# A decoder layer's state-space scan: input products one unit further ahead, units in another order

## The chip, the core and the metric

The kernel runs on one core of a Trainium2 chip. The core has a matrix engine (PE, TensorE), three elementwise engines (DVE or VectorE, ACT or ScalarE, POOL or GpSimd), and SP (SyncE), which here only issues transfers. Each engine works through its own instructions in order, and semaphores make one wait for another. SBUF and PSUM are the on-chip memories of 128 partitions[...]. The metric is the device time of one execution in microseconds. The kernel before took 1646.77 us, the median of 3 runs (1646.59 to 1649.17).

## The reference

One decoder layer on 4 sequences ("batches") of 512 positions and 512 features, in float32. It has three residual parts: a Mamba block, an int8-like quantized expert ("xattn") per sequence, and a mixture of 16 experts with a shared one. The change touches the Mamba block, whose core is a recurrence over time for 1024 channels with 16 states each:

```python
delta = softplus(einsum('dr,blr->bld', dt_proj_weight, dt) + dt_proj_bias)
A = -exp(A_log)
def step(h, inputs):
    d_t, B_t, C_t, u_t = inputs
    dA = exp(d_t[..., None] * A)
    h = h * dA + (d_t * u_t)[..., None] * B_t[:, None, :]
    y = einsum('bdn,bn->bd', h, C_t)
    return (h, y)
...
y = ys + u * D
y = y * silu(z)
return einsum('md,bld->blm', out_proj_weight, y)
```

Here u is a short convolution and silu of the first half of an input projection, z its second half, and dt, B and C are projections of u.

## The kernel before

**Units.** The 1024 channels of a batch go in NC = 8 chunks of 128 (`c`). In a chunk a *unit* `(g, p)` is the work on one of NG = 4 groups of states (4 states each) and on one half `p` of the chunk, that is two quarters of 32 channels. 32 channels by 4 states fill the 128 partitions; the two quarters lie beside each other, so that a unit is 128 partitions by 2 x 512 positions. A chunk has NU = 8 units, a batch 64, the kernel 256. `UNITS` (line 39) is their order: before, the pair of groups 0 and 1 on half 0, then both on half 1, then groups 2 and 3 likewise.

**What a unit does.** `spread` (690) copies delta and delta*u of a half from the tile `dd` to a tile `rep`, 32 rows to 128, by two transfers of 512 KB on SP; there are three rep buffers. `unit_inputs` (701) makes, on ACT, the decays `da` (two exponentials into PSUM, two buffers) and, on POOL, the product `bu` of B and delta*u (two buffers). `unit_scan` (714) is the recurrence itself, one scan on DVE over `da` and `bu`. `unit_out` (720) multiplies by C on DVE into a tile `h` (five buffers). `state_sums` (727) sums the 4 states of each channel by small matmuls with a 0/1 matrix `sel` into the PSUM tile `py`, which a matmul with the `skip` matrix (u*D) opens. `gated` (756) multiplies py by the gate `gzl` of the chunk, which `gate` (750) has loaded.

**Order of the work.** `scan_batch` (1653) writes the instructions slot by slot, a slot for each unit n. At its start it writes the inputs of unit n+1; at n = 4 the skip matmul and the sums of groups 0 and 1, at n = 0 those of groups 2 and 3 of the chunk before, whose `gated` follows at n = 1. Then come the scan, the output and, in three places (`more`, before the scan, before the output, and at the end of the slot), steps of the work beside.

**The work beside.** It is written as generators whose steps say what they wait for: `delta` (650, softplus for the chunk after next; four POOL operations of 128x512), `front` (475, layer norm, input projection, convolution and gates of the next batch; on POOL three additions a chunk at 502), the gates of batch 0 (`first_gates`, 613), the `back` of the batch before (763: output projection, quantized expert, shared expert and routing), and in the last batch the experts. The class `Pace` (133) keeps a clock for each engine while the instructions are being written. `clear` (222) lets a step be written only if its engine's clock is at most `BEHIND` past DVE's, and its inputs are ready at most `SLACK` past it; the calls before the scan and before the output add 3500 and 1200 ns for engines other than DVE. For POOL, SLACK is -300 and BEHIND 500 ns.

**Deadlines.** The list `copies` holds the rep halves to come: half 1 of the next chunk from n = 5, half 0 of the chunk after it from n = 7. A half is spread once its delta is over, and at n = 6 (half 0) and n = 7 (half 1) a delta that is not over is forced: `end` (1637) writes its steps until it is. The skip matrix of the chunk after next is loaded at n = 5. In the last chunk of a batch the tiles `bc` (B and C of a group, one buffer each) are loaded for the next batch, groups 0 and 1 at n = 4 and groups 2 and 3 at n = 7. Transfers on SP are issued in the order written, and one that must wait for its buffer holds those behind it.

Of the kernel before, what the change touches and what calls it, by code (L numbers as in the profile page):

```python
# [8 lines left out]
F32 = mybir.dt.float32  # L9
# [10 lines left out]
P = 128  # L20
B = 4
L = 512
# [4 lines left out]
NC = DI // P  # L27
# [3 lines left out]
CH = 32  # L31
# [4 lines left out]
NP = 2  # L36
NU = NG * NQC // NP

UNITS = [(g + i, p) for g in range(0, NG, 2) for p in range(NQC // NP) for i in range(2)]

GROUPS = [(0, 2), (2, 2)]

# [90 lines left out]
class Pace:  # L133
# [6 lines left out]
    TABLES = {"Exp": 0, "Tanh": 0, "Silu": 1, "Ln": 2}  # L140


    SLACK = {"DVE": 200, "Activation": 700, "Pool": -300, "PE": 3500, "SP": 500}
    BEHIND = {"DVE": 0, "Activation": 1500, "Pool": 500, "PE": 5000, "SP": 4000}

    def __init__(self, nc):
        self.nc, self.seen, self.table, self.queue = nc, 0, None, 0
# [95 lines left out]
def following(b, c, n):  # L243

    return (b, c + n) if c + n < NC else (b + 1, c + n - NC)
# [24 lines left out]
class Kernel:  # L270
# [271 lines left out]
    def first_front(self, sb, bank):  # L542

        nc, st = self.nc, self.state[0]
        xnT = self.xnT0
        for j in range(4):
            self.load_win(0, sb, j)
        for _ in self.layernormed(0, sb, bank, xnT):
            pass
        nc.sync.dma_start(self.wx_sb, self.wx)  # L550
        nc.sync.dma_start(self.wdt_sb, self.wdt)
        pj = {}
        pdt = bank.take([P, L])
        pbc = bank.take([P, L])


        pairs = [(b, self.fsideT[b], 0, k) for b in range(B) for k in (0, 2)]
        pairs += [(b, self.ctxwT[b], NK, 0) for b in range(B)]
        each = -(-len(pairs) // NC)
        held = {}  # L560

        def columns(c):
            for i in range(c * each, min((c + 1) * each, len(pairs))):
                b, w, _, k = pairs[i]
                held[i] = self.sb.tile([P, NP, L], F32, name="h", bufs=5)
                nc.sync.dma_start(held[i], w[k * P : (k + 2) * P, :].rearrange("(k p) n -> p k n", k=2))

        def largest(c):
            for i in range(c * each, min((c + 1) * each, len(pairs))):
                b, _, first, k = pairs[i]  # L570
                out = self.amw[:, b, first + k : first + k + 2]
                nc.vector.tensor_reduce(out, held.pop(i), AX.X, ALU.max, apply_absolute_value=True)

        def product(c):
            pj[c] = self.in_proj(0, bank, xnT, c)
            self.load_win(0, sb, c + 4)
            columns(c)

        def conv(c):
            cw = self.convw_sb  # L580
            u = self.u_tile(0, c)
            nc.scalar.activation(u, pj[c], AF.Copy, scale=cw[:, c, DC - 1 : DC])
            for j in range(1, DC):
                nc.vector.scalar_tensor_tensor(
                    u[:, j:], pj[c][:, : L - j], cw[:, c, DC - 1 - j : DC - j], u[:, j:], ALU.mult, ALU.add
                )
            bank.done(pj[c])

        def silu(c):
            nc.scalar.activation(st["u"][c], st["u"][c], AF.Silu, scale=2.0)  # L590
            largest(c)

        def sums(c):
            self.x_proj_of(st, pdt, 0, c)
            self.x_proj_of(st, pbc[: 2 * DS], 1, c)

        for _ in staged(range(NC), product, conv, silu, nothing, sums):
            pass
        flat = self.amw.rearrange("p b k -> p (b k)")
        nc.vector.reciprocal(flat, flat)  # L600
        nc.gpsimd.tensor_scalar_min(flat, flat, 1.0 / EPS_Q)
        st["dt"] = self.sb.tile([P, L], F32, name="dt", bufs=1)
        nc.scalar.copy(st["dt"], pdt)
        bank.done(pdt)
        rows = sb.tile([2 * DS, L], F32, name="rows", bufs=1)
        nc.scalar.copy(rows, pbc[: 2 * DS])
        bank.done(pbc)
        nc.sync.dma_start(self.rows_d[0], rows)
        self.done.add(("rows", 0))
        for g in range(NG):  # L610
            self.scan_bc(0, g)
# [86 lines left out]
            )  # L698
        st["rep"][c, p] = rep

    def unit_inputs(self, b, c, n):

        nc, st = self.nc, self.state[b]
        g, p = UNITS[n]
        rep = st["rep"][c, p]
        da = self.pscan.tile([P, NP, L], F32, name="da", bufs=2)
        for i in range(NP):
            q = c * NQC + p * NP + i
            nc.scalar.activation(da[:, i, :], rep[:, i, 0, :], AF.Exp, scale=self.a_sb[:, q, g : g + 1])  # L709
        bu = self.sb.tile([P, NP, L], F32, name="bu", bufs=2)  # L710
        nc.gpsimd.tensor_mul(bu, st["bc"][0, g].unsqueeze(1).to_broadcast([P, NP, L]), rep[:, :, 1, :])  # L711
        st["da"][c, n], st["bu"][c, n] = da, bu

    def unit_scan(self, b, c, n):
        st = self.state[b]
# [4 lines left out]
    def unit_out(self, b, c, n):  # L720
        st = self.state[b]
        g, p = UNITS[n]
        h = self.sb.tile([P, NP, L], F32, name="h", bufs=5)
        self.nc.vector.tensor_mul(h, st["da"].pop((c, n)), st["bc"][1, g].unsqueeze(1).to_broadcast([P, NP, L]))  # L724
        st["h"][c, g, p] = h

    def state_sums(self, b, c, g0):

        nc, st = self.nc, self.state[b]
        if g0 == 0:  # L730
            st["py"] = self.pscan.tile([P, L], F32, name="py", bufs=1)
            nc.tensor.matmul(st["py"], self.skips.pop((b, c)), st["u"][c], start=True, stop=False)
        py = st["py"]
        for g in range(g0, g0 + 2):
            for q in range(NQC):
                nc.tensor.matmul(  # L736
                    py[q * CH : (q + 1) * CH, :],
                    self.sel,
                    st["h"][c, g, q // NP][:, q % NP, :],
                    start=False,  # L740
                    stop=(g == NG - 1),
                )

    def skip(self, b, c):

# [799 lines left out]
    def run(self, ctx):  # L1545
# [21 lines left out]
        with tc.tile_pool(name="front", bufs=2) as fsb:  # L1567
            self.fsb = fsb
            self.first = ExitStack()
            sb = self.first.enter_context(tc.tile_pool(name="first", bufs=1))  # L1570
            self.xnT0 = sb.tile([P, NK, L], F32, name="xnT0", bufs=1)
            self.bank.add(self.pscan, "py")
            self.first_front(sb, self.bank)
            self.bank.names.remove((self.pscan, "py"))
            self.deltas, self.copies = {}, []
            for c in range(2):
                self.steps_of(0, c)
                self.skip(0, c)
            self.end(self.deltas[0, 0])
            for p in range(NQC // NP):  # L1580
                self.spread(0, 0, p)
            self.copies.append((0, 1, 0))
            self.fronts = Steps(self.pace, (w for b in range(1, B) for w in self.front(b)))
            self.unit_inputs(0, 0, 0)
            pool = ctx.enter_context(ExitStack())
            routed = Steps(self.pace, self.first_experts())
            backs = Steps(self.pace, self.backs(pool))
            backs.due = lambda slot: BACK_STEPS * (slot - NC * NU) / DUE
            self.fronts.due = lambda slot: FRONT_STEPS * slot / DUE
            self.scan_batch(0, [Steps(self.pace, self.first_gates(sb))])  # L1590
            for b in range(1, B - 1):
                self.scan_batch(b, [backs])
            assert self.fronts.over
# [52 lines left out]
    def finish(self, b, n):  # L1646

        if n == 0:
            self.state_sums(b, NC - 1, NG // 2)
        elif n == 1:  # L1650
            self.gated(b, NC - 1)

    def scan_batch(self, b, beside):

        self.started.add(b)
        for i in range(NC * NU):
# [3 lines left out]

            nb, nc = following(b, c, (n + 1) // NU)
            if nb < B:
                self.unit_inputs(nb, nc, (n + 1) % NU)

            if n == 4:
                self.state_sums(b, c, 0)
            if n == 0 and c:
                self.state_sums(b, c - 1, NG // 2)
            if b and not c:
                self.finish(b - 1, n)  # L1670
            self.more(beside, 3500)
# [3 lines left out]
            self.more(beside, 1200)  # L1675
            self.unit_out(b, c, n)
            if n == 2:
                self.gate(b, c)
                self.steps_of(*following(b, c, 2))

            if n == 5:
                self.skip(*following(b, c, 2))
                self.copies.append((*following(b, c, 1), 1))
            if n == 7:
                self.copies.append((*following(b, c, 2), 0))
            while self.copies:
                db, dc, p = self.copies[0]
                if db < B:
                    late = (db, dc) == following(b, c, 1) and n == NU - 2 + p or (db, dc) == (b, c)
                    if late:  # L1690
                        self.end(self.deltas[db, dc], [*self.deltas.values(), self.fronts, *beside])
                    elif not self.deltas[db, dc].over or self.pace.ready(self.state[db]["dd", dc]) > self.pace.engine["DVE"]:
                        break
                    self.spread(db, dc, p)
                self.copies.pop(0)
            if b + 1 < B and c == NC - 1 and n in (4, 7):
                for g in range(2):
                    self.scan_bc(b + 1, g + (n == 7) * 2)
            self.more(beside, 0)
# [67 lines left out]
```

## Time and profile before

All times are microseconds.

| what | value |
|---|---|
| median of 3 runs | 1646.77 |
| the profiled execution's own time | 1661.86 |
| its span, first to last instruction | 1659.9 |
| mean granted TensorE clock (share of full speed) | 0.844 |
| first scan starts, last scan starts | 90.7, 1335.0 |
| scans begin in batch 0, 1, 2, 3 | 90.7, 353.6, 671.9, 998.6 |
| DVE busy, 88 to 345 (257 long) | 231.3 |
| POOL busy, 88 to 345 | 228.8 |
| DVE busy, 345 to 680, 680 to 1010, 1010 to 1340 | 271.2, 275.3, 271.5 |
| POOL busy, the same stretches | 264.3, 248.2, 235.3 |
| DVE and POOL busy, 1340 to 1660 | 108.2, 143.3 |

The profile is of one execution, so sums are made against its own span. Its groups of instructions are given by line, engine and tile, as out<-in; "idle before" is the time that the engine stood idle just before such an instruction, with what ended the wait. Idle time of an engine that doesn't set the end costs nothing. In the rows of slices the span is cut in 40 equal parts, and a digit is the busy share in tenths. The page's chain of waits covers only the last 38 us, after which it finds no earlier link; it says nothing of the scan stage.

### The profile page before, as it was taken

To read this page: it belongs to the slowest core of one execution; us is meant where nothing else is said; L and a number is where in the kernel's file an instruction comes from. 1 tells how busy PE (TensorE), PEld (TensorE's weight loads), DVE (VectorE), ACT (ScalarE), POOL (GpSimd) and SP (SyncE) were. 2 spreads that over 40 slices of the span, in tenths; PEclk is the share of its full clock that TensorE was granted. 3 is DMA by queue.
4 is the path that set the end of the run, shared out by engine and by line. 5 is a ranking of instruction groups with operands and counts; after the bars stand their busy time and mean duration, and the time that the engine had idled before them with its cause. 6 is when DMAs were issued, how large, how long until landed. Compare 5 with 4: busy or idle time off the path is not lost. (4 is left out here: it accounts for less than half of the span.)

```text
span 1659.9 us, 15722 instructions
## 1 busy us (share of the span) xinstructions
PE 1207.7 (73%) x4552; PEld 584.8 (35%) x4552; DVE 1193.2 (72%) x1250; ACT 941.3 (57%) x1592; POOL 1130.7 (68%) x940
## 2 busy tenths in 40 slices
PE   6848777557866767898867885866667899668980
PEld 2213222112332323333423432343424347434760
DVE  4369999898867888778878898877778934352312
ACT  3376786755757778555787762567575414520330
POOL 1178999886767988676787874777788644126464
PEclk9978888768877887899978897987777999868995
DMA  5575655675233556665335658555567464168956
GB/s 192 154 162 126 141 110 111 130 189 110 74 90 78 135 120 163 161 203 143 78 84 127 172 137 293 138 158 133 130 184 204 120 260 146 65 230 292 342 213 216
DMA packets 109658, 262.22 MB, mean 158 GB/s; under 512 B 16192, under 2 KB 20416, under 8 KB 109504
## 3 DMA queue, kind: packets, MB, share of 16 engines
q1 hardware_dynamic: 93120, 204.50, 47.4%
q0 software_dynamic: 16448, 56.65, 9.8%
q8 instruction: 40, 0.66, 0.2%
q14 instruction: 50, 0.41, 0.1%
HBM read 168.55 MB, written 45.88 MB: 129 GB/s over the span
## 5 line engine op out<-in xcount | busy, mean ns | idle before, releaser
L711 POOL TENSOR_TENSOR bu<-bc,rep 128x1024 f32<-128x1024 f32 x256 | 602.2, 2358 | 169.8 <-DVE da L718 140.2
L718 DVE TENSOR_TENSOR_SCAN da<-da,bu 128x1024 f32<-128x1024 f32 x256 | 586.2, 2290 | 105.2 <-POOL bu L711 74.4
L709 ACT ACTIVATE da<-rep,a_sb 128x512 f32<-128x512 f32 x512 | 352.7, 690 | 261.2 <-DVE h L724 229.4
L724 DVE TENSOR_TENSOR h<-da,bc 128x1024 f32<-128x1024 f32 x256 | 312.3, 1220 | 19.6 <-PE py L736 9.2
L736 PE MATMUL py<-h,sel 128*32 128x512 f32 x1024 | 166.1, 687 | 50.2 <-DVE h L724 50.1
L1223 POOL DMA_INDIRECT wx<-in_wexp,wrow x62 | 63.0, 1016 | 79.9 <-PE bank L1513 22.9
L446 PE MATMUL bank_g<-xnT,win 128*128 128x512 f32 x192 | 100.2, 670 | 8.6 <-ACT tap L498 6.0
L502 POOL TENSOR_TENSOR u<-u,tap 128x511 f32<-128x511 f32 (+2 forms) x72 | 91.3, 1268 | 18.1 <-ACT tap L498 15.9
L446 PE MATMUL bank_b<-xnT,win 128*128 128x512 f32 x160 | 82.1, 661 | 24.6 <-ACT sp_r L669 15.2
L736 PEld LDWEIGHTS py<-h,sel 128*32 128x32 f32 x1024 | 31.1, 119 | 164.4 <-issue 83.3
L1467 POOL DMA_INDIRECT xs<-xn_d,tok x62 | 64.3, 1038 | 20.9 <-issue 19.2
L446 PE MATMUL bank_a<-xnT,win 128*128 128x512 f32 x128 | 63.2, 640 | 3.0 <-DVE gz L411 2.4
L446 PEld LDWEIGHTS bank_g<-xnT,win 128*128 128x128 f32 x192 | 40.5, 219 | 63.0 <-issue 51.2
L446 PEld LDWEIGHTS bank_b<-xnT,win 128*128 128x128 f32 x160 | 32.9, 213 | 72.9 <-issue 38.5
L680 POOL TENSOR_TENSOR sp_e<-sp_e,dd 128x512 f32<-128x512 f32 x32 | 40.7, 1272 | 26.2 <-ACT dd L675 26.1
L1261 POOL DMA_INDIRECT yg<-y_d,pos x32 | 33.3, 1041 | 23.9 <-DMA y_d<-ys 9.5
L1504 ACT ACTIVATE hs<-bank 128x128 f32<-128x128 f32 x24 | 6.6, 276 | 67.5 <-PE bank L1498 36.5
L1271 DVE SCALAR_TENSOR_TENSOR xr<-yg,topw,xr 128x512 f32<-128x512 f32 x32 | 23.7, 750 | 28.8 <-DMA yg<-y_d,pos 28.5
L791 PE MATMUL bank_b<-wout,u 128*128 128x512 f32 x64 | 36.1, 724 | 10.7 <-ACT tap L498 6.2
L1498 PE MATMUL bank<-xT,wx 128*128 128x128 f32 x352 | 43.1, 276 | 0.6 <-issue 0.6
L1498 PEld LDWEIGHTS bank<-xT,wx 128*128 128x128 f32 x352 | 41.3, 192 | 4.3 <-issue 3.5
L411 DVE SCALAR_TENSOR_TENSOR hs<-hs,bank 128x128 f32<-128x128 f32 x24 | 6.8, 284 | 50.1 <-ACT hs L1504 35.7
(422 smaller groups left out, 2439.4 us busy)
## 6 DMA issues: line engine op xcount, KB each, us to landing
rep<-dd SPq DMA_DIRECT2D x128, 512.0 KB
win<-in_win SPq DMA_DIRECT2D x64, 256.0 KB
x<-xr SPq DMA_DIRECT2D x48, 256.0 KB
xr<-x SPq DMA_DIRECT2D x48, 256.0 KB
y_d<-ys SPq DMA_DIRECT2D x48, 256.0 KB
bc<-rows_d SPq DMA_DIRECT2D x32, 256.0 KB
gz_d<-gz SPq DMA_DIRECT2D x32, 256.0 KB
gzl<-gz_d SPq DMA_DIRECT2D x32, 256.0 KB
```

The lines of the kernel that those rows point to most:

```text
L446: nc.tensor.matmul(pj, win[:, k, :], xnT[:, k, :], start=(k == 0), stop=(k == NK - 1))
L502: nc.gpsimd.tensor_add(u[:, j:], u[:, j:], v[j][:, j:])
L680: nc.gpsimd.tensor_sub(e, e, du)
L709: nc.scalar.activation(da[:, i, :], rep[:, i, 0, :], AF.Exp, scale=self.a_sb[:, q, g : g + 1])
L711: nc.gpsimd.tensor_mul(bu, st["bc"][0, g].unsqueeze(1).to_broadcast([P, NP, L]), rep[:, :, 1, :])
L718: self.nc.vector.tensor_tensor_scan(daf, daf, buf, 0.0, ALU.mult, ALU.add)
L724: self.nc.vector.tensor_mul(h, st["da"].pop((c, n)), st["bc"][1, g].unsqueeze(1).to_broadcast([P, NP, L]))
L736: nc.tensor.matmul(py[q * CH : (q + 1) * CH, :], self.sel, st["h"][c, g, q // NP][:, q % NP, :], start=False, stop=(g == NG - 1),)
L791: nc.tensor.matmul(po[t], st["u"][c][:, t * P : (t + 1) * P], wout[c], start=(c == part[0]), stop=(c == part[-1]),)
L1223: nc.gpsimd.indirect_dma_start(out=ws[s], out_offset=None, in_=self.wexp, in_offset=bass.IndirectOffsetOnAxis(ap=wrow[:, s : s + 1], axis= ...
L1467: nc.gpsimd.indirect_dma_start(out=xs[s], out_offset=None, in_=xn_d, in_offset=bass.IndirectOffsetOnAxis(ap=tok[:, s : s + 1], axis=0), bo ...
L1498: nc.tensor.matmul(ph[:, i, :], w[:, o : o + P], xT[:, k, :], start=(k == 0), stop=(k == NK - 1))
```

## The change

The order of units becomes group by group, each on both halves. `unit_inputs` is split: `unit_decays` (ACT) still runs one unit ahead; `unit_products` (POOL) runs two ahead, in three bu buffers. h has four buffers instead of five, each tile of the same 4 KB a partition. The sums of a group are written at the second slot after its first unit (n = 2, 4, 6, and n = 0 of the next chunk). The planner's two numbers for POOL are raised. Deadlines move: late deltas are forced at n = 5 and 6, half 0 of the chunk after next is listed from n = 6, and half 1 at n = 5 as before; the bc tiles of groups 0 and 1 are loaded at n = 3. Two loops write the steps on which a load depends until they are done: gates of batch 0, and `rows` of the next batch.

```diff
-UNITS = [(g + i, p) for g in range(0, NG, 2) for p in range(NQC // NP) for i in range(2)]
+UNITS = [(g, p) for g in range(NG) for p in range(NQC // NP)]
...
-    SLACK = {"DVE": 200, "Activation": 700, "Pool": -300, "PE": 3500, "SP": 500}
-    BEHIND = {"DVE": 0, "Activation": 1500, "Pool": 500, "PE": 5000, "SP": 4000}
+    SLACK = {"DVE": 200, "Activation": 700, "Pool": 2500, "PE": 3500, "SP": 500}
+    BEHIND = {"DVE": 0, "Activation": 1500, "Pool": 3500, "PE": 5000, "SP": 4000}
...
-                held[i] = self.sb.tile([P, NP, L], F32, name="h", bufs=5)
+                held[i] = self.sb.tile([P, NP, L], F32, name="h", bufs=4)
...
-    def unit_inputs(self, b, c, n):
+    def unit_decays(self, b, c, n):
...
-        bu = self.sb.tile([P, NP, L], F32, name="bu", bufs=2)
-        nc.gpsimd.tensor_mul(bu, st["bc"][0, g].unsqueeze(1).to_broadcast([P, NP, L]), rep[:, :, 1, :])
-        st["da"][c, n], st["bu"][c, n] = da, bu
+        st["da"][c, n] = da
+
+    def unit_products(self, b, c, n):
+        nc, st = self.nc, self.state[b]
+        g, p = UNITS[n]
+        bu = self.sb.tile([P, NP, L], F32, name="bu", bufs=3)
+        nc.gpsimd.tensor_mul(
+            bu, st["bc"][0, g].unsqueeze(1).to_broadcast([P, NP, L]), st["rep"][c, p][:, :, 1, :]
+        )
+        st["bu"][c, n] = bu
...
-        h = self.sb.tile([P, NP, L], F32, name="h", bufs=5)
+        h = self.sb.tile([P, NP, L], F32, name="h", bufs=4)
...
-    def state_sums(self, b, c, g0):
+    def state_sums(self, b, c, i):
...
-        for g in range(g0, g0 + 2):
-            for q in range(NQC):
...
+        for q in range(NQC):
+            h = st["h"][c, i, q // NP][:, q % NP, :]
+            nc.tensor.matmul(py[q * CH : (q + 1) * CH, :], self.sel, h, start=False, stop=(i == NG - 1))
...
-            self.unit_inputs(0, 0, 0)
+            self.unit_decays(0, 0, 0)
+            for n in range(2):
+                self.unit_products(0, 0, n)
...
-                self.unit_inputs(nb, nc, (n + 1) % NU)
-
-            if n == 4:
-                self.state_sums(b, c, 0)
+                self.unit_decays(nb, nc, (n + 1) % NU)
+            nb, nc = following(b, c, (n + 2) // NU)
+            if nb < B:
+                self.unit_products(nb, nc, (n + 2) % NU)
+
+            if n and n % 2 == 0:
+                self.state_sums(b, c, n // 2 - 1)
             if n == 0 and c:
-                self.state_sums(b, c - 1, NG // 2)
+                self.state_sums(b, c - 1, NG - 1)
...
             if n == 2:
+                while b == 0 and ("gate", b, c) not in self.done:
+                    beside[0].go()
...
             if n == 5:
+                self.copies.append((*following(b, c, 1), 1))
                 self.skip(*following(b, c, 2))
-                self.copies.append((*following(b, c, 1), 1))
-            if n == 7:
+            if n == 6:
                 self.copies.append((*following(b, c, 2), 0))
...
-                    late = (db, dc) == following(b, c, 1) and n == NU - 2 + p or (db, dc) == (b, c)
+                    late = (db, dc) == following(b, c, 1) and n == NU - 3 + p or (db, dc) == (b, c)
...
-            if b + 1 < B and c == NC - 1 and n in (4, 7):
+            if b + 1 < B and c == NC - 1 and n in (3, 7):
+                while ("rows", b + 1) not in self.done:
+                    self.fronts.go()
```

More of the change, by code (lines that the diff above doesn't have):

```diff
@@ L722, in unit_out @@
         g, p = UNITS[n]
-        h = self.sb.tile([P, NP, L], F32, name="h", bufs=5)
+        h = self.sb.tile([P, NP, L], F32, name="h", bufs=4)
         self.nc.vector.tensor_mul(h, st["da"].pop((c, n)), st["bc"][1, g].unsqueeze(1).to_broadcast([P, NP, L]))
         st["h"][c, g, p] = h
-    def state_sums(self, b, c, g0):
+    def state_sums(self, b, c, i):
         nc, st = self.nc, self.state[b]
-        if g0 == 0:
+        if i == 0:
             st["py"] = self.pscan.tile([P, L], F32, name="py", bufs=1)
@@ L733, in state_sums @@
         py = st["py"]
-        for g in range(g0, g0 + 2):
-            for q in range(NQC):
[L736 to L742, printed above, removed]
+        for q in range(NQC):
+            h = st["h"][c, i, q // NP][:, q % NP, :]
+            nc.tensor.matmul(py[q * CH : (q + 1) * CH, :], self.sel, h, start=False, stop=(i == NG - 1))
     def skip(self, b, c):
@@ L1648, in finish @@
         if n == 0:
-            self.state_sums(b, NC - 1, NG // 2)
+            self.state_sums(b, NC - 1, NG - 1)
         elif n == 1:
```

## The prediction

> **What bounds the kernel now.** I read the busy shares first, then the slices, then the groups with their idle time, then the table of who waited for whom, and last the timeline around single waits.
>
> ```profile
> PE 1207.7 (73%) x4552; PEld 584.8 (35%) x4552; DVE 1193.2 (72%) x1250; ACT 941.3 (57%) x1592; POOL 1130.7 (68%) x940
> ...
> DVE  4369999898867888778878898877778934352312
> ...
> POOL 1178999886767988676787874777788644126464
> ...
> L711 POOL TENSOR_TENSOR bu<-bc,rep 128x1024 f32<-128x1024 f32 x256 | 602.2, 2358 | 169.8 <-DVE da L718 140.2
> L718 DVE TENSOR_TENSOR_SCAN da<-da,bu 128x1024 f32<-128x1024 f32 x256 | 586.2, 2290 | 105.2 <-POOL bu L711 74.4
> ...
> L724 DVE TENSOR_TENSOR h<-da,bc 128x1024 f32<-128x1024 f32 x256 | 312.3, 1220 | 19.6 <-PE py L736 9.2
> ```
>
> The scan stage runs from the first scan at 90.7 us to the last at 1335.0 us, three quarters of the span. A unit costs DVE 2.29 + 1.22 = 3.51 us, 256 of them 898.6 us. Summed over 88 to 1340 us, 1252 us long, DVE is busy 1049.2, POOL 976.5, PE 913.9, ACT 824.9. So DVE sets the stage, and what can be won is in its 203 us of idle time. From the starts of the scans the four batches take 263, 318, 327 and 340 us: 4.1 us a unit in batch 0, 5.0 to 5.3 after.
>
> ```profile
> ACT da L709 <- DVE h L724: 229.4, 109, 11.7
> POOL bu L711 <- DVE da L718: 140.2, 78, 10.3
> ...
> DVE da L718 <- POOL bu L711: 74.4, 29, 27.4
> ...
> DVE da L718 <- ACT da L709: 29.4, 17, 4.4
> ...
> POOL bu L711 <- DMA rep<-dd: 25.2, 6, 9.2
> ```
>
> These rows are total, number, longest. POOL waits 78 times for a free bu buffer, and all the same DVE waits 29 times for bu: POOL is early on the average and late at times, which is what a deeper buffer is for. But the 74.4 us are not all to be had. I took each of these scans from the timelines and asked when the decays of the same unit were ready. Where bu came last DVE lost 69.4 us; decays alone would have kept 39.7 of them, 25.6 at the very first scan (the wait of 27.4, for the first rep) and 9.9 at 472.40 us. The other cases leave **26 us: 9 in batch 0, in bits of 0.3 to 1.7, and 17 after it**, of which 5.3 are at 1146.77 and 0.9 at 1244.45.
>
> **The change part by part.**
>
> *Products two ahead.* The 256 products stay, at 2.36 us; each is issued a slot earlier, past the POOL side work of that slot. The bound is 0 to −26 us. The planner's own allowance tells how much of the small waits goes. Before, ahead of a scan it lets POOL stand 3.5 + 0.5 us past DVE and then writes one more addition (1.27) and the product (2.36): 7.6 us, against two units of 3.51, so 0.6 us late. That is what the trace has in batch 0 (waits of 0.50, 0.53, 0.55, 0.60, 0.62, 0.69). After: 3.5 + 3.5 + 1.27 + 2.36 = 10.6 against 10.5, 0.1 late. I take 7 of batch 0's 9, and half of the later 17, whose causes are stalls in POOL's own queue, which the wider SLACK (2.5 us for an input not yet ready, where it was −0.3) also makes likelier. **−15.5 us.**
>
> Here a rule of the Trainium skill speaks against the change. "Perfetto Trace Analysis", section "Identifying the Most-Contended Engine", has the engine of the highest occupancy worked on first. That is PE or DVE here, and the change takes no instruction from either: by the rule the sum is 0. By the waits, DVE's gaps are ended by an engine with 68% occupancy, and −15.5 stands. I go by the rows, since occupancy doesn't tell which engine is late.
>
> *Four buffers for h, sums every two units.* DVE's waits for h on the sums are 9.2 us in three places (0.72, 3.11, 5.35), all at unit 5 of a chunk, one slot after the eight sums were written. Now a reused h has its sums two slots back; a slot more is 3.5 us at least, and 8.8 at the longest. All three go: **−9** (bound 0 to −9.2). PE pays: 64 more groups, each with a bubble (0.76 us in the timeline ahead of the first sum), 49 us, beside 338 us of PE idle in the stage. PE is near full (56.6 of 60 us) only from 720 to 780: 49 × 60/1252 = **+2.4**. And PE, which runs in order, sits at the sums until DVE's h is done: 50.1 us of matmul idle now, at 64 places, then at 128. Behind it stand the in_proj and back products, and DVE waits for such products (all but py) for 48 us in the stage. Bounds 0 and +48; most of this work is written only when it is due, so near the low end: **+5**. In the startup two h tiles a step are loaded; with four buffers each load would find its buffer already read (the loads at 31.03 reuse what was reduced by 30.6): 0, since the margin is 0.4 us at its least; if it fails, a win load behind them on SP waits about a microsecond.
>
> *Units by state group.* Both halves of rep are now in use to the end of a chunk. Half 1 of the next chunk takes the buffer of half 0, whose last reader was unit 5 and is now unit 6; and it is first read by unit 1, whose product is written in slot 7, where it was unit 2, in slot 1 of the next chunk. So its transfer starts a slot later and is wanted two slots sooner. I call T5 the start of scan 5. Unit 6's two decays (1.42 us) run after h of unit 4, so the buffer is free at T5 + 1.5.
>
> ```profile
> 460.93 7.81 SPq L696 DMA_DIRECT2D rep<-dd  x4
> ...
> 468.11 0.69 ACT L709 ACTIVATE da<-rep,a_sb 128x512 f32<-128x512 f32 x1 [9.59 <-DMA rep<-dd]
> 469.94 2.02 ACT L709 ACTIVATE da<-rep,a_sb 128x512 f32<-128x512 f32 x3 [1.14 <-DMA rep<-dd]
> ...
> 472.40 2.30 DVE L718 TENSOR_TENSOR_SCAN da<-da,bu 128x1024 f32<-128x1024 f32 x1 [11.64 <-POOL bu L711]
> ```
>
> In this timeline (start, duration, operation, idle before it and what ended it) a half is whole 9.0 us after its issue; two more cases that POOL waited for give 9.4 and 10.4 (issues 1250.5 and 625.3, products 1259.88 and 635.71). Then the product: ready at T5 + 1.5 + 9.0..10.4 + 2.4 = T5 + 12.9 to 14.3. Scan 1 of the next chunk is at T5 + 4 slots: 16.4 us in batch 0, over 20 later. The room is **2.1 to 3.5 us in batch 0 and 6 to 8 us after**. "DMA: Bandwidth & Descriptors", section "Specifications", gives 435 GB/s as the ceiling into SBUF: an estimate from it for the 1.05 MB is 2.4 us, and some 8 us of room even in batch 0. The rows say four times that, and decide: the half comes just in time. Old issues of half 1 lie in slots 4 and 5 but for four later ones out of 32; each of those I charge a microsecond: **+4**, bounds 0 and +22 (below).
>
> SP is also rid of a wait: the skip load ahead of half 1 waited for the chunk's skip matmul, now two slots sooner.
>
> ```profile
> SPq L748 <- PE py L732: 67.8, 15, 14.4
> ```
>
> *Deadlines.* A late delta is forced at the end of slot 5 for half 0, was 6. The stall at 472.40 came of it: transfer in slot 7. One slot sooner takes 4 to 5 us off: **−5** (0 to −11). At startup unit 1 needs half 1, there at 93.81, plus its product 2.36: 96.2 instead of 95.38, **+0.8**. The bc loads a slot sooner wait on SP for h of unit 3 up to a slot, three times in all, with two slots of room for the reader: 0, up to +5 if SP's queue behind them holds a rep. The two new loops (gate in batch 0, rows) do nothing where the step is done: rows left at slots 50, 56 and 49 of their batches, wanted at 59: 0 (but see rival B). Decays stay one ahead, so DVE's 29.4 us on ACT stay.
>
> *Sum*: −15.5 − 9 + 2.4 + 5 + 4 − 5 + 0.8 = **−17.3 us** on the profiled execution, 1661.9 us with 2 us around its span, which is 0.9% above the runs' median. Scaled: 1646.8 − 17.1 = **1630 us**. The tail after 1340 us waits for the last batch in any case, so the gain passes through to it.
>
> **The rivals.**
>
> A, *rep half 1 becomes the wait* (slower). Place: SP's queue ahead of that transfer in slots 5 and 6, where the win loads stand. SP's waits for PE's in_proj before a win load are 40 with a total of 239 us, 6.0 each. If one of these stands ahead of half 1 at each chunk end, batch 0 loses 7 × (6.0 − 2.8) = 22 us, the others nothing: −15 + 22 gives about 1655 us. Nothing is left of the gain from 5 us of delay on; beyond 7 us the 24 later chunks pay too. For it: the room worked out above. Against it: in batch 0 half 1 left SP at 212.4, 245.7 and 279.0, just as its buffer came free, with SP waiting for nothing else.
>
> B, *forced side work*: with PE held at the sums, the front or the gates of batch 0 come late, and the loops write steps that are not ready, on which the in-order engines sit. For it: such loops cost only where a schedule misses its deadlines, and rows of batch 2 had three slots to spare. Some 10 us at each of three batch ends, less half the gain: 1662 us.
>
> C, *the lead is spent*: the planner fills it with POOL work that waits for its inputs, and ACT's decays, one ahead, end the waits that bu ended. 0 of the 15.5, the rest as above: −2, 1645 us.
>
> **Numbers.** A measurement here tells some 0.2% (3.3 us) from no change. Forecast 0.48, A 0.22, B 0.17, C 0.13 (0.09 within 0.2%, 0.04 slower by unlisted costs). Faster 0.48, same 0.09, slower 0.43. The forecast's own range is 1612 (all 26 and the 11) to 1643 (POOL a quarter, PE +20). With A to C: 1610 to 1668; that leaves out a strong A with over 8 us of delay and B at its worst.
>
> **What would show it.** POOL's bu row: idle before it on DVE's scan falls from 140, DVE's wait for bu falls from 74 to under 50, its wait for h on py to about 0. PE's wait at the sums grows past 50. POOL's wait for rep rises from 25; if it passes 60 with DVE's scans at unit 1 of a chunk behind it, A holds. DVE's wait on ACT's decays over 40 would be C. Batch 0 should take about 256 us instead of 263. It is wrong if batch 0 gets longer, or if the scan stage shortens and the tail after the last scan grows by as much.

## The result, and the profile after

The changed kernel took 1696.3 us (median of 4, 1691.7 to 1703.9), the kernel before 1646.8: a ratio of **1.030, interval 1.027 to 1.033**. Forecast was 1630, range 1610 to 1668. It is slower by 49.5 us. The profiled execution's span is 1689.6 us.

The page of the changed kernel: slices of DVE, then the groups that answer to those shown of before.

```profile
DVE  4379898989798788879567785987787853344412
...
L717 POOL TENSOR_TENSOR bu<-bc,rep 128x1024 f32<-128x1024 f32 x256 | 600.0, 2356 | 207.6 <-DMA rep<-dd 115.3
L726 DVE TENSOR_TENSOR_SCAN da<-da,bu 128x1024 f32<-128x1024 f32 x256 | 586.2, 2290 | 103.9 <-ACT da L709 55.0
...
L732 DVE TENSOR_TENSOR h<-da,bc 128x1024 f32<-128x1024 f32 x256 | 312.5, 1221 | 14.3 <-PE py L744 2.1
L744 PE MATMUL py<-h,sel 128*32 128x512 f32 x1024 | 211.2, 733 | 96.2 <-DVE h L732 96.0
```

And the row of the sums in the kernel before:

```profile
L736 PE MATMUL py<-h,sel 128*32 128x512 f32 x1024 | 166.1, 687 | 50.2 <-DVE h L724 50.1
```

On DVE and POOL the same work takes the same busy time, while PE's sums, now in twice as many groups, are busy 45 us longer. What has changed most is who ends the waits. POOL used to wait for scans (140.2 us), which is being early; now it waits most for the copied halves `rep`. The scans used to wait most for bu and now do for the decays. The table of waits (total, times, longest) of the same kernel:

```profile
POOL bu L717 <- DMA rep<-dd: 115.3, 27, 13.4
POOL bu L717 <- DVE da L726: 77.2, 29, 10.1
...
DVE da L726 <- ACT da L709: 55.0, 35, 4.7
DVE da L726 <- POOL bu L717: 46.4, 12, 27.3
...
ACT da L709 <- DMA rep<-dd: 36.3, 16, 9.4
```

From the first scan to the last output the stage went from 1249.0 to 1296.5 us; DVE's idle time in it rose by 43.4, and what comes after it shrank by 16.4 in the profiled executions. The batches took 268, 306, 358 and 364 us: batch 1 won 12 us, batch 0 lost 5, and batches 2 and 3 lost 55. The two profiled executions lie 30 us apart, less than the medians: that of before was 15 us above its median, that of the changed kernel 5 below.

### The profile page after: what moved, and what is told of

It is laid out like the page before. It is cut to its first block, busy times and chain, and to the rows that moved or that the text cites. A ratio compares the mean times of both kernels' runs of the same rounds, so it can differ in the third digit from the quotient of the medians.

```text
span 1689.6 us, 15734 instructions
## 1 busy us (share of the span) xinstructions
PE 1251.4 (74%) x4552; PEld 583.5 (35%) x4552; DVE 1197.9 (71%) x1250; ACT 942.9 (56%) x1592; POOL 1127.3 (67%) x940
## 5 line engine op out<-in xcount | busy, mean ns | idle before, releaser
L717 POOL TENSOR_TENSOR bu<-bc,rep 128x1024 f32<-128x1024 f32 x256 | 600.0, 2356 | 207.6 <-DMA rep<-dd 115.3
L744 PE MATMUL py<-h,sel 128*32 128x512 f32 x1024 | 211.2, 733 | 96.2 <-DVE h L732 96.0
L446 PE MATMUL bank_g<-xnT,win 128*128 128x512 f32 x168 | 89.3, 681 | 8.4 <-ACT sp_r L669 5.1
L446 PE MATMUL bank_a<-xnT,win 128*128 128x512 f32 x168 | 80.2, 622 | 1.2 <-DVE gz L411 0.5
L446 PE MATMUL bank_b<-xnT,win 128*128 128x512 f32 x144 | 76.5, 680 | 1.6 <-DVE gz L411 1.6
L446 PEld LDWEIGHTS bank_g<-xnT,win 128*128 128x128 f32 x168 | 35.3, 220 | 61.3 <-issue 44.8
L740 PE MATMUL py<-u,skip 128*128 128x512 f32 x64 | 41.5, 736 | 17.0 <-DVE u L760 13.0
L446 PEld LDWEIGHTS bank_a<-xnT,win 128*128 128x128 f32 x168 | 31.9, 197 | 45.1 <-issue 37.0
L686 POOL TENSOR_TENSOR dd<-dd,u 128x512 f32<-128x512 f32 x32 | 40.7, 1271 | 2.0
L682 POOL TENSOR_TENSOR sp_e<-sp_e,sp_r 128x512 f32<-128x512 f32 x32 | 40.6, 1268 | 1.4
```

What stands on the lines that cost most here:

```text
L446: nc.tensor.matmul(pj, win[:, k, :], xnT[:, k, :], start=(k == 0), stop=(k == NK - 1))
L744: nc.tensor.matmul(py[q * CH : (q + 1) * CH, :], self.sel, h, start=False, stop=(i == NG - 1))
```

## Experiments

All ratios are against the kernel before, run on the same chip in the same rounds. There it took 1646 to 1649 us, but 1663 to 1665 in the rounds of the first four experiments and of the last two (in the table, *sums* at HOP 120 and at LATE 110). That a ratio means the same in both was not tested.

### First four: one part at a time

Theories: *planner* (the raised numbers), *sums* (PE is held at twice as many places), *rep* (half 1 comes late in the new order).

The kernel before with the two changed lines for SLACK and BEHIND, and nothing else:

> The kernel before with only POOL's two planner numbers raised (SLACK 2500, BEHIND 3500); products one ahead, old order, eight sums at a time. Theory planner (the raised numbers let POOL's queue fill with work that waits): most of the 49 us, 1680 or more, POOL's lateness at the scan over 100 us where it was 74. Theory sums (PE is held at twice as many places): below 1665, since the sums are where they were. Theory rep (half 1 comes late in the new order): below 1665. With one product ahead some loss is expected of all, as a lead of 3.5 us is given to POOL that it has no buffer for.

Measured 1.0247 (1.0202 to 1.0293). The time fits the planner theory; the scan's wait for bu rose from 74 to 93 us, less than it asked.

The opposite edit in the changed kernel:

> The changed kernel with POOL's two planner numbers as before (-300, 500). Theory planner: most comes back, 1660 or less. Theory sums: 1685 to 1700, PE's wait for h at the sums still near 96 us. Theory rep: 1685 to 1700, POOL's wait for rep still over 80 us.

Measured 1.0356 (1.0316 to 1.0395), so taking the raised numbers back doesn't help. The signs of the other two theories both stayed: POOL waited 129.4 us for rep, and PE 105.0 us for h at the sums.

The changed kernel with eight sums at a time:

```diff
...
-            if n and n % 2 == 0:
-                self.state_sums(b, c, n // 2 - 1)
+            if n == 4:
+                for i in range(2):
+                    self.state_sums(b, c, i)
             if n == 0 and c:
-                self.state_sums(b, c - 1, NG - 1)
+                for i in range(2, NG):
+                    self.state_sums(b, c - 1, i)
```

> The changed kernel with the sums of two groups written together, at n = 4 and at n = 0 of the next chunk, as before; h keeps four buffers. Theory sums: DVE's waits for the products of the back fall by some 30 us and the time to about 1660, less what the four h buffers take at unit 4 (its output now waits for sums written in its own slot: about 1 us a chunk, 30 us at the most). Theory rep: 1690 or more. Theory planner: 1690 or more.

Measured 1.0457 (1.0419 to 1.0496). This line of its waits explains why it is not a clean test: four h buffers want the sums every two units, or else the output of unit 4 waits, here for 84.8 us in all.

```profile
DVE h L732 <- PE py L744: 84.8, 31, 8.1
```

The kernel before with the sums of each two units:

```diff
+        for g, p in UNITS[2 * i : 2 * i + 2]:
+            for j in range(NP):
+                q = p * NP + j
...
-            if n == 4:
-                self.state_sums(b, c, 0)
+            if n and n % 2 == 0:
+                self.state_sums(b, c, n // 2 - 1)
...
```

> The kernel before with the sums of each two units written at n = 2, 4, 6 and 0; nothing else. Theory sums: slower by 25 to 45 us, PE's wait for h at the sums (50 us in matmuls) about doubled, DVE's waits for back products up by 30. Theories rep and planner: within 10 us of 1647.

Measured 1.0319 (1.028 to 1.0358). That looks like the sums theory at once. But four kernels with edits of four kinds, two of them opposite, had all come out 2.5 to 4.6% above the kernel before, so I suspected what they share: each makes the planner place all the side work anew.

### The planner alone

```diff
-    HOP = 120
+    HOP = 130
```

> The kernel before with the planner's constant HOP (its guess of the time between an engine's end and another's start) at 130 ns instead of 120; no buffer, order, sum or limit differs, only where the side work falls. Four edits of quite different kinds cost 40 to 75 us each, so a fourth theory stands beside the others, plan: the side work's placement is planned with a clock model, the kernel before is a lucky or fitted placement, and any edit that makes the planner place anew loses some 30 to 60 us of it, whatever the edit is for. Theory plan: 25 us slower or more. Theories sums, rep and planner numbers: within 8 us of the kernel before.

> The same with HOP at 110 ns. Theory plan: 15 to 60 us slower, not the same amount as at 130. The other theories: within 8 us of the kernel before.

> The kernel before with the planner's constant LATE (how much a step that is overdue may run late, per step) at 110 ns instead of 100. Theory plan: 10 to 60 us slower. The other theories: within 8 us.

> The changed kernel with HOP at 130 ns. Theory plan: this is another draw of the same kind as the changed kernel, so within 25 us of it, either side, and not 50 us slower than it, as it has no fitted placement to lose. The other theories: within 8 us of the changed kernel.

Measured 1.0092, 1.0055 and 1.0148 for the kernel before, and 1.0126 for the changed one, which is 1.7% below what it has at HOP 120. A constant that changes no buffer and no dependency moves the time by 0.5 to 1.7%. For the kernel before, the plan theory had the sign right, and the size too large at both HOP values and right at LATE 110. The changed kernel moved by some 29 us, a little more than the 25 that it had allowed. So one run of a design can't tell 1% of its own from its placement, and the rest of the runs make a table: designs against four settings of the planner.

### Designs at four settings

The designs: the kernel before; *sums* (with sums of each two units); *old order* (sums, products two ahead in three buffers, four h buffers, raised numbers, but the units in their old order, with half 0 forced at n = 5, half 1 at n = 7, and the other deadlines as before); and the changed kernel, which has the new order with its deadlines on top. The edit of *old order* beside the kernel before, other than those of the change:

```diff
-                    late = (db, dc) == following(b, c, 1) and n == NU - 2 + p or (db, dc) == (b, c)
+                    late = (db, dc) == following(b, c, 1) and n == NU - 3 + 2 * p or (db, dc) == (b, c)
```

> The changed kernel with HOP at 110 ns. With HOP 130 the two kernels are 1.0092 (before) and 1.0126 (changed) of the kernel before as it stands. Theory plan: the changed kernel is one draw of a spread of about 1.00 to 1.03, and this is another: 1.005 to 1.025, beside 1.0055 of the kernel before at the same HOP. Theory sums: the change costs of itself, by PE's waits at twice as many places, so 1.02 to 1.04 again, and the 1.0126 was the lucky draw.

> The changed kernel with LATE at 110 ns. Theory plan: 1.00 to 1.03 of the kernel before, within 0.015 of the 1.0148 that the kernel before has at the same LATE. Theory sums: 0.015 or more above it.

> The kernel before with the sums of each two units, and HOP at 130 ns. At HOP 120 it was 1.0319. Theory sums: 1.025 or more again, 0.016 above the kernel before at this HOP. Theory plan: 1.00 to 1.02.

> The old order of units with all else of the change: products two ahead in three buffers, four h buffers, sums each two units, the raised planner numbers; half 0 forced at n = 5, half 1 at n = 7. Theory rep: POOL's wait for rep back under 50 us from 115 and the kernel 15 us or more faster than the changed one. Theory plan: anywhere from 1.00 to 1.03, POOL's wait for rep lower all the same. Theory sums: 1.02 or more.

> Old order with all else of the change, at HOP 130. The changed kernel has 1.0126 here. Theory rep (the new order costs of itself): 0.01 or more below that, POOL's wait for rep under 50 us where the changed kernel has 118. Theory plan: anywhere from 0.995 to 1.025, with no system against the changed kernel.

> The same at HOP 110, where the changed kernel has 1.0172. Theory rep: 1.007 or less, POOL's wait for rep under 50 us (126 in the changed kernel). Theory plan: anywhere from 0.995 to 1.025.

> The same at LATE 110, where the changed kernel has 1.0180. Theory rep: 1.008 or less. Theory plan: anywhere from 0.995 to 1.025.

> The kernel before with the sums of each two units, at HOP 110, where the kernel before has 1.0055. Its draws so far are 1.0319 and 1.0041. Theory sums: 1.015 or more. Theory plan: 1.00 to 1.03, and the mean of the four within 0.01 of the mean of the kernel before.

> The kernel before with the sums of each two units, at LATE 110, where the kernel before has 1.0148. Theory sums: 1.025 or more. Theory plan: 1.00 to 1.03.

| design | HOP 120 | HOP 130 | HOP 110 | LATE 110 | mean |
|---|---|---|---|---|---|
| before | 1 | 1.0092 (1.0060-1.0125) | 1.0055 (1.0037-1.0074) | 1.0148 (1.0117-1.0178) | 1.0074 |
| sums | 1.0319 (1.0280-1.0358) | 1.0041 (1.0023-1.0058) | 1.0031 (1.0017-1.0045) | 1.0057 (1.0033-1.0081) | 1.0112 |
| old order | 0.9954 (0.9941-0.9967) | 0.9999 (0.9984-1.0015) | 0.9917 (0.9888-0.9946) | 0.9928 (0.9901-0.9955) | 0.9950 |
| changed | 1.0304 (1.0273-1.0334) | 1.0126 (1.0090-1.0161) | 1.0172 (1.0139-1.0206) | 1.0180 (1.0142-1.0217) | 1.0196 |

The differences down a column, at the four settings: sums less before +3.2, -0.5, -0.2, -0.9%: no cost of its own that this can show, and the 1.0319 is put down to its placement. Old order less sums -3.7, -0.4, -1.1, -1.3%: **the lead with its numbers gains, mean -1.6%**, or -0.9% without the pair at HOP 120, whose 1.0319 stands apart (this step also takes the fifth h buffer away and forces half 0 at n = 5). Changed less old order +3.5, +1.3, +2.6, +2.5%: **the new order with its deadlines loses, mean +2.5%, some 40 us**, with one sign everywhere. The forecasts of the rep theory for *old order* all came true.

Means over the four profiles of each design, in the scan stage (us; POOL's wait for the very first product is left out, and the last row leaves out what waits for py):

| | before | sums | old order | changed |
|---|---|---|---|---|
| stage, first scan to last output | 1262.0 | 1265.7 | 1236.2 | 1278.5 |
| DVE idle in it | 211.0 | 214.0 | 185.9 | 226.9 |
| POOL's product waits for rep | 24.8 | 20.3 | 24.9 | 105.6 |
| scan waits for bu | 76.5 | 78.5 | 34.8 | 49.6 |
| scan waits for the decays | 28.1 | 27.1 | 42.7 | 46.5 |
| DVE's side work waits for POOL | 19.3 | 13.2 | 13.6 | 24.1 |
| DVE's side work waits for PE | 61.6 | 77.6 | 77.1 | 83.1 |

Between the last two columns POOL waits 81 us more for rep. The growth is at unit 1, the first to read half 1 in the new order: there POOL waits 77 to 100 us in the four profiles of the changed kernel, and at most 1.1 in those of *old order* (7 to 16 at its unit 2, which reads half 1 first there). DVE's idle time grows by 41 us. Its waits for POOL make 25 of them, 14.8 at the scans and 10.4 in side work; 3.8 more are at the decays, 6.1 in side work that waits for PE, and some 4 in side work that waits for ACT. That each of the 25 comes of a wait for rep was not followed one by one. The two designs also differ in how the sums fall on PE, and with it in the granted TensorE clock (last section); the PE row shows 6 us at most of it.

The waits of *old order* at HOP 120:

```profile
POOL bu L717 <- DVE da L726: 113.4, 53, 14.3
...
DVE da L726 <- ACT da L709: 49.1, 28, 4.6
DVE da L726 <- POOL bu L717: 36.6, 5, 27.3
POOL bu L717 <- DMA rep<-dd: 31.4, 12, 9.1
```

Of the 36.6 us that scans still wait for bu, 27.3 are the first scan's. What a deeper buffer can give here is had.

One part was left in this: the raised numbers.

> Old order, products two ahead in three buffers, four h buffers, sums each two units, but POOL's planner numbers as before (-300, 500). With the raised numbers it was 0.9954. If the raised numbers carry the gain: 1.01 or more, with the additions of the front late. If the lead carries it: 0.99 to 1.005. A single draw of the planner, so a difference under 0.01 tells nothing.

Measured 1.0099 (1.0064 to 1.0133) against 0.9954, so the lead without the numbers seems to lose what it gains; the numbers without the lead gave 1.0247. That fits a pair that belongs together, but each is a single placement, and *sums* alone spread over 2.9%: it stays open.

A direct test of the rep theory, the changed kernel with a fourth rep buffer, wants another 8 KB a partition, which SBUF does not have left, and was not tried. That the order with its deadlines costs is shown; that rep is how is read from the waits.

**A version that beats both**: the old order with the rest of the change, at HOP 110: 0.9917 of the kernel before (0.9888 to 0.9946), 1631.5 us. It is the best of four settings; the design's mean is 0.9950.

## Why the prediction was wrong

**The step that failed is the one on units by state group, "+4, bounds 0 and +22"**, with the 5 us that the earlier deadline was to give back. The runs give some +40 us. The timing in that step nearly held. In the changed kernel at HOP 120 half 1's first transfer leaves SP 2.9 us after scan 5 starts (median of 31 chunks; 1.5 was worked out), and the tile's own view has the landing of each transfer:

```profile
DMA to landing us min/median/max: 6.6/8.2/11.1
```

Unit 1's product starts 9.6 us after that issue (median), as the 9.0 to 10.4 said. Its scan waited for it in four chunks, 5.2 us in all (3.1 to 8.8 us in the four profiles of the design), so +4 was about right for what it priced. But POOL mostly stands ready and takes the half as it lands: of its 115.3 us of waiting for rep, 79.9 are at unit 1, in 21 of the 32 chunks, and 35.4 at unit 0, of which 9.1 at the very start. I priced only whether *that product* would be late for *its scan*. I did not price what stands behind it in POOL's queue.

What holds the transfer is mostly half 0's buffer, which unit 6's decays are the last to read. SP's own waits for it, before and then in the changed kernel:

```profile
SPq L696 <- ACT da L709: 39.9, 17, 6.7
...
SPq L696 <- ACT da L709: 134.0, 23, 14.3
```

Other transfers stand behind these waits; what that costs was not separated. The timelines of the changed kernel at the turn from chunk 3 to chunk 4 of batch 2 (start, duration, operation, idle before and its releaser), SP, POOL, DVE and ACT in turn:

```profile
814.31 7.70 SPq L696 DMA_DIRECT2D rep<-dd  x4
...
814.19 0.10 POOL L688 MEMSET dd<- 128x1 f32 x1
823.27 2.34 POOL L717 TENSOR_TENSOR bu<-bc,rep 128x1024 f32<-128x1024 f32 x1 [8.98 <-DMA rep<-dd]
829.49 2.34 POOL L717 TENSOR_TENSOR bu<-bc,rep 128x1024 f32<-128x1024 f32 x1 [3.88 <-DMA rep<-dd]
831.90 0.24 POOL L914 TENSOR_SCALAR amx<-amx 128x4 f32<-128x4 f32 x1
...
833.64 0.22 POOL L917 TENSOR_SCALAR s<-s 128x4 f32<-128x4 f32 x1
...
825.64 2.30 DVE L726 TENSOR_TENSOR_SCAN da<-da,bu 128x1024 f32<-128x1024 f32 x1 [7.66 <-POOL bu L717]
827.85 0.67 DVE L411 SCALAR_TENSOR_TENSOR u<-bank_a,u 128x512 f32<-128x512 f32 x1
833.90 0.18 DVE L919 RECIPROCAL rs<-s 128x4 f32<-128x4 f32 x1 [5.37 <-POOL s L917]
833.99 1.21 DVE L732 TENSOR_TENSOR h<-da,bc 128x1024 f32<-128x1024 f32 x1
...
837.07 2.29 DVE L726 TENSOR_TENSOR_SCAN da<-da,bu 128x1024 f32<-128x1024 f32 x1
...
833.90 1.28 ACT L924 ACTIVATE ds<-ident,s 128x128 f32<-128x128 f32 x4 [2.60 <-POOL s L917]
```

Delta came late, so the four transfers of both halves left SP one behind the other from 814.31 on. The scan of unit 0 lost 7.66 us on half 0; the stall of the kernel before at 472.40 is of this kind, though it had none at this turn. New is what follows. Unit 1's product stands at the head of POOL's queue until half 1 lands, at 829.49, though its scan comes only at 837.07. Behind it are four operations for the quantized expert, 2 us in all; DVE waits 5.37 us for the last of them at 833.90, with the output of unit 0 queued behind, and ACT waits as well. In the old order units 0 and 1 are both on half 0, and POOL would not have met half 1 here. So rival A had the right wait, but not its place or its price: it looked for the delay in SP's queue behind the win loads, and counted stalls of the scan at a chunk's end, not of POOL's queue.

The other steps:

- *Products two ahead, -15.5*: the scan's wait for bu went from 74.4 to 46.4 us, of 47 that are not the first scan's to 19. In the table the step gives -1.6%, or -27 us, but only -0.9%, or 16 us, without the pair at HOP 120, so it can't be told from the -15.5. Of the 43.7 us that the scans no longer wait for bu, ACT's decays took 15.6 back. That is rival C's mechanism, at a third of the gain; in the changed kernel at HOP 120 its sign, over 40 us on the decays, came true with 55.0.
- *h and sums, -9 + 2.4 + 5*: h waits fell from 9.2 to 2.1 us. DVE's waits for side products of PE rose by 15 to 21 us with the sums, where I had 5 of a bound of 48; PE's matmuls waited 96 us for h instead of 50. In the time the sums come to +0.4%, lost in the scatter.
- *Deadlines, -5*: not seen; the stall above is of the very kind, and POOL waited another 13.4 us for half 0 at 742.84, where the longest such wait of the kernel before was 9.2.
- *Rival B*: rows left at slots 53, 57 and 49 of their batches, before the loop at 59, so that loop wrote nothing. The loop for the gates of batch 0 wrote two steps, in the first chunk only; DVE waits there 1.34 us for ACT's gate at 103.66.
- *Not in the sum at all*: placement. The kernel before lies 0.7% below the mean of its own four settings, the changed kernel 1.1% above the mean of its. With the design's 1.2% (+0.4 - 1.6 + 2.5 and rounding) this makes the 3.0%. By these four settings, less than half of the measured loss is the change's own.
- *Signs*: POOL's wait for scans fell to 77.2 us, the scan's wait for bu to 46.4, and PE's at the sums rose, as said. Batch 0 got longer, which was named as a sign of being wrong.
- *Sums that don't come out*: the transfer estimate of 2.4 us would leave some 10 us of room in batch 0, not 8 (16.4 - 1.5 - 2.4 - 2.4). The upper end of the forecast's own range comes to over 1650 by its terms, not 1643, and rival B to about 1668, not 1662. And "by the rule the sum is 0" says too much, since filling DVE's gaps is work on DVE, one of the two engines that it names.

## What to carry to other kernels

Work that is issued further ahead moves its waits ahead too: on an in-order engine ask not only whether the early instruction is in time for its own reader, but what is queued behind it while it waits for its input. A lead is worth having only where the inputs are there as early; here keeping the order that reads the late half one unit later turned a loss of 2% into a gain of 0.5% (means of four settings). And where a planner places the work, run each design at several settings of a constant that should not matter before believing a difference of a per cent or two.

## What was not expected of the hardware

The mean granted TensorE clock goes with how the sums fall on PE. In the designs whose four sums hit two quarters of py twice (*sums*, *old order*) it was 0.869 to 0.881 in all nine profiles; in those whose four hit four quarters (before, changed, and the first three experiments) 0.830 to 0.848 in all eleven. The time didn't follow it: *sums* has the higher clock and is no faster than before. Why the clock goes with it was not tested.

The starts of the matmuls differ too. In a group of four that hits four quarters they lie 7 ns apart (medians of the traces of before and of the changed kernel), so the four overlap. Where two quarters are hit twice they lie 7, 446 and 7 ns apart (*old order*, HOP 120): the second pair starts well after the first. The busy time of the sums is 278.9 us there, against 211.2 in the changed kernel:

```profile
L745 PE MATMUL py<-h,sel 128*32 128x512 f32 x1024 | 278.9, 681 | 54.9 <-DVE h L732 54.5
```

So *old order* is the faster one although its sums keep PE busy longer.
